# Lookup steps counted by their share of a tile, T1 issued half a slot sooner, blended values written out by ScalarE

## The chip, the cores and the metric

One core of a Trainium2 chip runs the kernel. The metric is the device time of one execution in microseconds (us), as the median of several runs. The engines are TensorE (PE, with its weight loads as PEld), VectorE (DVE), ScalarE (ACT), GpSimd (POOL) and SyncE (SP). DMAs are issued by an engine's queue: SPq is SP's, ACTq is ACT's.

## The reference

Eight sequences of 1024 tokens of width 512 are normalized, go through an attention with three decays and a gated FFN whose weights come out of a 16-entry table, and the product of both is added to the input.

```python
def attn(x, Wq, Wk, Wv, Wo, Wg, decay_logits, out_scale):
    q = x @ Wq
    gate = softmax(x @ Wg)
    expn, causal = maximum(diff - 1, 0), diff > 0      # diff: column minus row
    for i in range(3):
        k, v = x @ Wk[i], x @ Wv[i]
        w = sigmoid(decay_logits[i]) ** expn * causal
        retrieved = einsum('bts,bsd->btd', einsum('btd,bsd->bts', q, k) * w, v)
        blended = blended + gate[..., i:i + 1] * retrieved
    return blended @ Wo * out_scale

def ffn(x, lut, gate_idx, up_idx, down_idx):           # 512 -> 1376 -> 512
    h = silu(x @ lut[gate_idx].T) * (x @ lut[up_idx].T)
    return h @ lut[down_idx].T

xn = layernorm(x)                                      # x: (8, 1024, 512), float32
out = x + attn(xn, ...) * silu(ffn(xn, ...))
```

## The kernel before

Everything is float32. The kernel has two phases. Phase 1 (about the first 597 us) computes the attention up to its blended values and builds the FFN's weights. Phase 2 does the FFN as products in the manner of Strassen (seven products in place of eight, with sums of blocks ahead and behind), the output projection and the final sum; the change doesn't touch it.

**Phase 1 as a loop.** `phase_1` runs a batch counter b from 0 to 8 and in each b eight slots k from 0 to 7. A slot works on chunk c = 7 - k, 128 tokens; chunks go from the last to the first, because the state runs backwards in time. Three streams of work run side by side, each written as a Python generator whose yields mark the places where the other streams get their turn:

- `project(b)`, called newer (and ending for what is left of it in the next b): it loads x by chunk, takes the statistics (for b = 0 on DVE, L404 to L408, otherwise on ACT with junk outputs, L411 and L412, and POOL's power for rstd, L413 and L414), normalizes (L419 on DVE for b = 0, L421 and L422 on ACT otherwise), transposes into xnT (L427, copy L428), makes values pv (L434, copy L437), the gates by a softmax (L440 to L473), and the features q and k by Strassen-like products (`features`, L475 to L535). A gate goes to HBM and comes back spread over all partitions as the tile ga (L473).
- `chunks(b - 1)`, called older: the recurrent attention of the batch before. For each chunk: ga times q on DVE (L627) and qb = ga times a table on POOL (L631); transposes pk of the keys (L643); scores psc (L650) from ga; pr = psc times the decay table on DVE (L652); the state's update pu (L660); the blended output po (L674) from the state and qb, and from pr and the values; a copy of po into the tile bl (L675, ACT). After the eight chunks bl, 128x1024, goes to HBM (bld, L689). The pool of bl has one buffer, so the next batch's first copy waits for that DMA. PSUM tiles pt, pv, pk, psc and po share the three banks of pool p_c.
- `ffn_weights`, called weights: 17 tiles (eleven gate_up, one down_tail, five down). A tile loads its indices (L264 to L266, L317) and looks them up (`look_up`): three bits of the index (L218), the lowest bit spread over the word (L221), eight leaves that select between two table entries (L225), and seven predicated copies that merge them (L242), all on DVE. Then come four sums of 128x256 on POOL (L272 to L276), and for every second gate or down tile four sums over the pair, 128x896 each (L290, L292, L297, L300; L339 to L346). The tile wgu that the last leaf level writes has two buffers, and the pair sums read the wgu of both tiles. Results go to HBM through SP's queue (quadd, L298 and L301). The indices of the following tile are loaded one tile ahead.

In `features`, T1 is the difference of two blocks of xnT, `t1 = b12 - b11` (L505, DVE). T2, T3 and T4 are at L509, L514 and L520. The product pe (L495) reads T1.

**The order.** The generators' turns set the order in which instructions are traced, and for PE, DVE, ACT and POOL `keep_order` holds each engine to this order. SP's order is left to the scheduler. `defer(n, ...)` puts a DMA off by n calls of `tick`, of which a slot has three. `build_some(n)` draws n steps from weights, three times in each slot; before the change a step is one yield, whatever the instruction behind it costs. Yields with nothing between them (three behind a gate pair, eight behind a down pair) are pauses in the lookup.

Of the kernel before, what the change touches and what calls it, by code (L numbers as in the profile page):

```python
# [48 lines left out]
def recurrent_block(ctx: ExitStack, tc, x, wq, wk, wv, wo, wg, decay_logits, out_scale, lut, gidx, uidx, didx, out):  # L49
# [163 lines left out]
    def look_up(build, dst, iv, rows, n):  # L213

        bits = [build.tile([P, n], U8, name=f"bit{j}", tag=f"bit{j}") for j in (1, 2, 3)]
        low = iv.bitcast(U8).rearrange("p (n four) -> p n four", four=4)[:, :, 0]
        for j in (1, 2, 3):
            nc.vector.tensor_scalar(bits[j - 1][:rows, :n], low, 1 << j, None, ALU.bitwise_and)  # L218
            yield

        nc.vector.tensor_scalar(iv, iv, 31, 31, ALU.logical_shift_left, ALU.arith_shift_right)  # L221
        yield

        def leaf(o, k):
            nc.vector.tensor_scalar(  # L225
                o.bitcast(I32),
                iv,
                lut_x[:rows, k, :],
                lut_i[:rows, k, 0:1],
                ALU.bitwise_and,  # L230
                ALU.bitwise_xor,
            )

        def tree(o, level, k):
            if level == 0:
                leaf(o, k)
                yield
                return
            t = build.tile([P, n], F32, name=f"leaf{level}", tag=f"leaf{level}")
            yield from tree(o, level - 1, k)  # L240
            yield from tree(t[:rows, :n], level - 1, k + (1 << (level - 1)))
            nc.vector.copy_predicated(o, bits[level - 1][:rows, :n], t[:rows, :n])  # L242
            yield

        yield from tree(dst, 3, 0)

    def ffn_weights(build, pool, pair_pool):
# [9 lines left out]

        def gate_up(o):
# [8 lines left out]
            yield  # L267
# [6 lines left out]
            yield  # L274
# [16 lines left out]
            yield  # L291
            nc.gpsimd.tensor_tensor(pair[:, :, 1], pair[:, :, 0], b11, ALU.subtract)  # L292
            yield
            if o >= 4 * NQ:
                for _ in range(4):
                    yield
            nc.gpsimd.tensor_tensor(b21, b11, b21, ALU.subtract)  # L297
            defer(3, lambda: nc.sync.dma_start(out=to[:, :, 2:4, :], in_=low))  # L298
            yield
            nc.gpsimd.tensor_tensor(pair[:, :, 2], b12, pair[:, :, 1], ALU.subtract)  # L300
            defer(4, lambda: nc.sync.dma_start(out=to[:, :, 4:7, :], in_=pair))  # L301
            for _ in range(3):
                yield

        def down_tail():
# [3 lines left out]
            yield  # L309
# [4 lines left out]
        def down(rows, e, ends):  # L314
# [3 lines left out]
            yield  # L318
# [5 lines left out]
            yield  # L324
# [15 lines left out]
            yield  # L340
            nc.gpsimd.tensor_tensor(b12, b22, b12, ALU.subtract)
            defer(2, lambda: nc.sync.dma_start(out=to[:, :, 0:2, :], in_=up))
            yield
            nc.gpsimd.tensor_tensor(pair[:, :, 1], b22, pair[:, :, 0], ALU.subtract)
            yield
            nc.gpsimd.tensor_tensor(pair[:, :, 2], b21, pair[:, :, 1], ALU.subtract)  # L346
            defer(4, lambda: nc.sync.dma_start(out=to[:, :, 4:7, :], in_=pair))
            for _ in range(8):
                yield
# [4 lines left out]
        yield  # L354
# [22 lines left out]
    def project(b, pools, sides, kept):  # L377
# [97 lines left out]
        def features(hf):  # L475
# [5 lines left out]
            qk[hf] = att.tile([P, NI + 1, U], F32, name=f"qk{b}_{hf}", tag=f"qk{hf}", bufs=1)  # L481
            c11, c12, c21, c22 = (qk[hf][:, 2 * j : 2 * j + 2, ts(c, H)] for j in (0, 1) for c in (0, 1))
            ts_ = tp.tile([P, 4, 2, H], F32, name=f"ts{b}_{hf}", tag=f"ts{hf}")
            b11, b12, b21, b22 = (xnT[:, 2 * v : 2 * v + 2, ts(2 * hf + c, H)] for v in (0, 1) for c in (0, 1))
            t1, t2, t3, t4 = (ts_[:, k] for k in range(4))
            a11, a12, s3, a22 = (wqk_sb[:, 2 * v : 2 * v + 2, ts(j, 2 * D)] for j in (0, 1) for v in (0, 1))
# [18 lines left out]
            nc.vector.tensor_tensor(t1, b12, b11, ALU.subtract)  # L505
            yield
# [56 lines left out]
        for k in range(NC):  # L563
# [11 lines left out]
            if k == NC // 2:  # L575
# [3 lines left out]
                of_half = features(1)  # L579
                next(of_half)  # L580
# [8 lines left out]
            if k >= NC // 2:  # L589
                next(of_half, None)  # L590
            yield
        of_half = features(0)
        for k in range(NC // 2):
            yield
            if k == 0:
                next(of_half)
# [17 lines left out]
    def chunks(b, pools, kept):  # L614
# [74 lines left out]
        (nc.scalar if at_end else nc.sync).dma_start(out=bl_d[b], in_=bl)  # L689

    def phase_1():
        nonlocal small, p_a, p_c, p_r
        with (
# [22 lines left out]
            def build_some(n):  # L716
                for _ in range(n):
                    next(weights, None)
# [12 lines left out]
            for b in range(B + 1):  # L731
                following = project(b + 1, pools, sides, kept) if b + 1 < B else iter(())
                older = chunks(b - 1, (chk, blp), kept) if b else iter(())
                for k in range(NC):


                    if b == 0:
                        steps = (k > 0, k >= NC // 2, 2 * (k >= NC // 2))
                    elif b < B:
                        steps = ((1, 1, 4), (1, 2, 5), (1, 2, 4), (1, 2, 3))[k % 4]  # L740
                    else:
                        steps = (1, 0, 0)
# [7 lines left out]
                    build_some(steps[0])  # L750
# [6 lines left out]
                    build_some(steps[1])  # L757
                    next(older, None)
                    build_some(steps[2])
# [681 lines left out]
```

## Time and profile before

| | us |
|---|---|
| median of 3 runs | 2113.19 (2112.64 to 2113.54) |
| the profiled execution | 2114.02 |
| its span, first to last instruction | 2111.9 |
| DVE busy in 0 to 597 | 511.23 |
| PE busy in 0 to 597 | 581.45 |
| POOL busy in 0 to 597 | 301.82 |
| ACT busy in 0 to 597 | 373.91 |
| PE busy in 597 to 2112 | 1507.20 |

The profile is one execution on the chip. A time row such as `349.10 0.65 SPq L689 ...` gives the start and the length in us from the span's start, the engine, the line of the code, the operation and its operands as output<-input, and the number of instructions put together. In brackets stands how long the engine was idle before and what released it. A waits row gives engine, tile and line, what it waited for, then the total in us, how many times, and the longest. A group's row ends in busy us, mean ns, and idle time with its releasers.

The costliest groups of the lookup and its neighbours on DVE between 60 and 597 us, in groups of one shape, and of POOL before 597 us:

```profile
L242 DVE COPY_PREDICATED leaf<-bit,leaf 128x1024 f32<-128x1024 uint8 x56 | 81.8, 1460 | 1.2
L225 DVE TENSOR_SCALAR leaf<-idx,lut_x,lut_sb 128x1024 int32<-128x1024 int32 x97 | 81.4, 859 | 0.0
L627 DVE TENSOR_TENSOR ga<-ga,qk 128x384 f32<-128x384 f32 x61 | 44.5, 730 | 2.6 <-DMA ga<-gTd 2.6
L218 DVE TENSOR_SCALAR bit<-idx 128x1024 uint8<-128x1024 uint8 x39 | 40.2, 1068 | 0.0
L652 DVE TENSOR_TENSOR pr<-psc,w_tab 128x384 f32<-128x384 f32 x62 | 34.2, 552 | 36.2 <-PE psc L650 36.2
```

```profile
L631 POOL TENSOR_TENSOR qb<-ga,q_tab 128x384 f32<-128x384 f32 x56 | 79.0, 1410 | 55.0 <-DVE ga L627 49.0 <-PE pe L495 3.6 <-issue 1.7
L300 POOL TENSOR_TENSOR pair<-wgu,pair 128x896 f32<-128x896 f32 x5 | 11.9, 2380 | 0.0
L297 POOL TENSOR_TENSOR wgu<-wgu 128x896 f32<-128x896 f32 x5 | 11.1, 2216 | 0.0
L275 POOL TENSOR_TENSOR wgu<-wgu 128x256 f32<-128x256 f32 x10 | 11.2, 1120 | 0.0
```

### The profile page before, as it was taken

How to read it: one execution, taken by the hardware profiler on the slowest of the kernel's cores; microseconds unless marked ns; L12 is line 12 of the kernel's file. 1: busy time of each engine (PE TensorE's matmuls, PEld its weight loads, DVE VectorE, ACT ScalarE, POOL GpSimd, SP SyncE). 2: the span in 40 equal slices, each digit the busy share in tenths (PEclk: the TensorE clock that was granted, in tenths of full speed). 3: DMA queues.
4: the chain of work that ended last, by engine and by line, in shares of the span. 5: the costliest groups of instructions: out<-in, count | busy, mean ns of one | idle time of the engine just before them, and what ended most of it. 6: DMA issues, size and time to landing. Idle time of an engine off the chain costs nothing.

```text
span 2111.9 us, 32189 instructions
## 1 busy us (share of the span) xinstructions
PE 2088.6 (99%) x11691; PEld 1752.9 (83%) x11691; DVE 1444.2 (68%) x2214; ACT 943.6 (45%) x2116; POOL 1040.4 (49%) x1050
## 2 busy tenths in 40 slices
PE   9999999999999999999999999999999999999999
PEld 7877878888878888887878888887978888797877
DVE  8889897889735675575567556656755665675567
ACT  4766666676434424423441442344144324423531
POOL 4554564364445447516543751655275255527432
PEclk9999999999999999999999999999999999999999
DMA  8765779657864744464454446345544634464442
GB/s 217 146 180 165 188 176 199 161 153 138 157 204 150 256 155 159 162 223 142 157 196 174 157 147 245 136 155 173 197 160 151 248 123 153 160 223 147 150 155 108
DMA packets 184635, 361.51 MB, mean 171 GB/s; under 512 B 50927, under 2 KB 122238, under 8 KB 184478
## 3 DMA queue, kind: packets, MB, share of 16 engines
q1 hardware_dynamic: 169894, 335.20, 52.7%
q0 software_dynamic: 4480, 14.68, 1.7%
q10 hardware_dynamic: 10104, 9.58, 1.5%
q8 instruction: 93, 1.52, 0.3%
q14 instruction: 64, 0.52, 0.1%
HBM read 282.87 MB, written 76.55 MB: 170 GB/s over the span
## 4 chain that ended last, share of the span: by engine, by line
PE 76%; DVE 3%; DMA 1%; issue 0%; ACT 0%; SPq 0%; DVEq 0%; ACTq 0%
PE s L885 33%; PE sE L885 6%; PE s12d L1139 5%; PE s21d L1139 5%; PE s11d L1139 5%; PE fs L833 3%; PE pd L1252 3%; PE ps L1259 3%; PE sEd L1139 2%; PE fsE L833 1%; PE pv L434 1%; PE s11d L1150 1%; PE s21d L1150 1%; PE s12d L1150 1%; PE sEd L1150 1%; PE po L674 1%
## 5 line engine op out<-in xcount | busy, mean ns | idle before, releaser
L885 PE MATMUL s<-xs,wq 128*128 128x256 f32 x3264 | 731.2, 379 | 0.0
L885 PEld LDWEIGHTS s<-xs,wq 128*128 128x128 f32 x3264 | 619.5, 190 | 95.9 <-issue 8.4
L908 DVE TENSOR_TENSOR s<-s,e 128x512 f32<-128x512 f32 x136 | 95.1, 699 | 204.4 <-ACT s L907 204.3
L1223 POOL TENSOR_TENSOR cu<-cu 128x256 f32<-128x256 f32 x32 | 35.1, 1097 | 306.4 <-DVE cl L1222 306.4
L434 PE MATMUL pv<-wvg_sb,xnT 128*128 128x387 f32 x512 | 177.6, 488 | 0.0
L816 POOL TENSOR_TENSOR xs<-xs 128x256 f32<-128x256 f32 x224 | 170.9, 789 | 8.1 <-PE fs L833 3.5
L912 DVE TENSOR_TENSOR sE<-s,e 128x512 f32<-128x512 f32 x136 | 95.0, 698 | 104.6 <-PE s L885 104.6
L976 POOL TENSOR_TENSOR u<-u,e 128x512 f32<-128x512 f32 x64 | 79.9, 1270 | 148.8 <-DVE u L972 130.3
L903 ACT COPY e<-sE 128x512 f32<-128x512 f32 x136 | 79.6, 585 | 138.8 <-PE sE L885 138.5
L885 PE MATMUL sE<-xs,wq 128*128 128x256 f32 x544 | 139.6, 379 | 0.0
L434 PEld LDWEIGHTS pv<-wvg_sb,xnT 128*128 128x128 f32 x512 | 94.4, 191 | 53.9
L980 POOL TENSOR_TENSOR h<-h,u 128x512 f32<-128x512 f32 x64 | 80.1, 1272 | 112.9 <-DVE u L987 100.3
L896 ACT COPY s<-s 128x512 f32<-128x512 f32 x136 | 77.5, 570 | 109.0 <-PE s L885 106.7
L413 POOL TENSOR_SCALAR rstd<-rstd 128x1 f32<-128x1 f32 x56 | 28.8, 515 | 192.3 <-ACT junk L412 186.4
L907 ACT COPY s<-s 128x512 f32<-128x512 f32 x136 | 77.5, 570 | 98.1 <-PE s L885 98.1
L1139 PE MATMUL s12d<-wdd,z 128*128 128x128 f32 x896 | 118.5, 275 | 0.6 <-ACT s12d L1161 0.6
L885 PEld LDWEIGHTS sE<-xs,wq 128*128 128x128 f32 x544 | 103.4, 190 | 14.1
L1139 PEld LDWEIGHTS s12d<-wdd,z 128*128 128x128 f32 x896 | 109.0, 192 | 0.8 <-ACT s12d L1161 0.8
L631 POOL TENSOR_TENSOR qb<-ga,q_tab 128x384 f32<-128x384 f32 x56 | 79.0, 1410 | 55.0 <-DVE ga L627 49.0
L225 DVE TENSOR_SCALAR leaf<-idx,lut_x,lut_sb 128x1024 int32<-128x1024 int32 (+2 forms) x119 | 96.5, 832 | 0.0
L242 DVE COPY_PREDICATED leaf<-bit,leaf 128x1024 f32<-128x1024 uint8 (+2 forms) x68 | 94.2, 1385 | 1.5
L1263 POOL TENSOR_TENSOR gx<-gx,cu 128x512 f32<-128x512 f32 x32 | 40.7, 1277 | 82.0 <-DVE cu L1261 64.5
(263 smaller groups left out, 4534.2 us busy)
## 6 DMA issues: line engine op xcount, KB each, us to landing
wq<-quadd SPq DMA_DIRECT2D x112, 896.0 KB, 4.5
wdd<-wdd SPq DMA_DIRECT2D x56, 896.0 KB, 4.6
xs<-xsd SPq DMA_DIRECT2D x56, 512.0 KB, 6.1
wq<-quadd SPq DMA_DIRECT2D x48, 448.0 KB, 4.1
x<-in_x SPq DMA_DIRECT2D x64, 256.0 KB, 4.7
xsd<-ts SPq DMA_DIRECT2D x16, 1024.0 KB, 14.9
gx<-in_x SPq DMA_DIRECT2D x64, 256.0 KB, 5.3
out<-gx POOLq DMA_DIRECT2D x56, 256.0 KB, 2.3
```

The lines of the kernel that those rows point to most:

```text
L225: nc.vector.tensor_scalar(o.bitcast(I32), iv, lut_x[:rows, k, :], lut_i[:rows, k, 0:1], ALU.bitwise_and, ALU.bitwise_xor,)
L242: nc.vector.copy_predicated(o, bits[level - 1][:rows, :n], t[:rows, :n])
L434: nc.tensor.matmul(pv, lhsT=xnT[:, v, ts(c, P)], rhs=wvg_sb[:, v, :], start=(v == 0), stop=(v == NV - 1))
L816: nc.gpsimd.tensor_tensor(o, x1, x2, ALU.subtract)
L833: nc.tensor.matmul(ps, lhsT=w[:, 2 * W_OF[k] + n, :m], rhs=xs[:, X_OF[k], 2 * n : 2 * n + 2, :], start=start and n == 0, stop=stop and n == 1,
L885: nc.tensor.matmul(self.t[n][:, ts(a, H)], lhsT=self.w[:, a, (0, 1, 6, 3, 4, 5, 2)[i - 1], :], rhs=self.xs[:, X_OF[self.ks[a]], D_OF[i], : ...
L908: nc.vector.tensor_tensor(self.t[1], self.t[1], self.e, ALU.add)
L912: nc.vector.tensor_tensor(self.t[3], self.t[2], self.e, ALU.add)
L976: nc.gpsimd.tensor_tensor(o[:, n], o[:, n], other[:, n], ALU.add)
L980: nc.gpsimd.tensor_tensor(of_h(half, n), of_h(half, n), two(other[:, n]), ALU.mult)
L1139: nc.tensor.matmul(self.t[n][:, ts(a, P)], lhsT=self.lhs[i][:, e, ts(a, P)], rhs=self.w[:, e, D_OF[i], :], start=start and a == 0 and e == ...
L1150: nc.tensor.matmul(self.t[n][:, ts(a, P)], lhsT=self.left[:, ts(2 * (n // 2) + a, P)], rhs=wd_left[:, D_OF[self.k], ts(n % 2, P)], start=F ...
```

## The change

Three things change.

1. A yield of the lookup now carries a number, its share of a tile of 128x1024 (.04 for a bit or the spreading of the lowest, .045 for a leaf, .07 for a predicated copy, .07 or .14 for a POOL sum, nothing for loads). `build_some(part)` adds its part to what is due and draws steps until it is used up, and each of the three places in a slot has a part of its own, by k % 4. The empty yields behind the pairs are gone.
2. T1 and the creation of its tile move ahead of the creation of the feature tile qk, with a yield of their own; the first turn of `features`, which issues T1, is taken at the end of the slot before, so half a slot sooner. For the second half of a batch's features this is the end of the batch's last slot.
3. The DMA that writes bl out is issued by ACT for all batches; before, ACT issued it for the last batch alone, and SP for the other seven.

The number of instructions on PE, DVE, ACT and POOL is unchanged, apart from the DMA's issue. PE's order is the same. ACT's is the same but for the seven DMAs, each directly behind the batch's last copy into bl (L675), and one DMA of the down weights (L328) that comes a few places sooner. DVE's differs in 380 rows, POOL's in 96, and SP's in 106.

```diff
@@ -212,14 +212,18 @@
 
     def look_up(build, dst, iv, rows, n):
 
+        part = n / NB
         bits = [build.tile([P, n], U8, name=f"bit{j}", tag=f"bit{j}") for j in (1, 2, 3)]
         low = iv.bitcast(U8).rearrange("p (n four) -> p n four", four=4)[:, :, 0]
         for j in (1, 2, 3):
             nc.vector.tensor_scalar(bits[j - 1][:rows, :n], low, 1 << j, None, ALU.bitwise_and)
-            yield
+            yield 0.04 * part
 
         nc.vector.tensor_scalar(iv, iv, 31, 31, ALU.logical_shift_left, ALU.arith_shift_right)
-        yield
+        yield 0.04 * part
 
         def leaf(o, k):
             nc.vector.tensor_scalar(
@@ -234,13 +238,13 @@
         def tree(o, level, k):
             if level == 0:
                 leaf(o, k)
-                yield
+                yield 0.045 * part
                 return
             t = build.tile([P, n], F32, name=f"leaf{level}", tag=f"leaf{level}")
             yield from tree(o, level - 1, k)
             yield from tree(t[:rows, :n], level - 1, k + (1 << (level - 1)))
             nc.vector.copy_predicated(o, bits[level - 1][:rows, :n], t[:rows, :n])
-            yield
+            yield 0.07 * part
 
         yield from tree(dst, 3, 0)
 
@@ -254,6 +258,8 @@
 
         upper = []
+        SUM, WIDE_SUM = 0.07, 0.14
 
         def gate_up(o):
             s, m = OCH[o]
@@ -264,14 +270,14 @@
             nc.sync.dma_start(out=iv[:, 2:6, :], in_=gs)
             nc.sync.dma_start(out=iv[:, 0:2, :], in_=us[:, 0:2, :])
             nc.sync.dma_start(out=iv[:, 6:8, :], in_=us[:, 2:4, :])
-            yield
+            yield 0.0
             wf = pool.tile([P, 2 * NB], F32, name="wgu", tag="wgu", bufs=2)
             yield from look_up(build, wf[:, :n], idx[:, :n], P, n)
             w = wf[:, : 2 * n].rearrange("p (k two m) -> p k two m", two=2, m=m)
             a21, a11, a12, a22, s1, s2, s3, s4 = (w[:, k] for k in range(8))
             nc.gpsimd.tensor_tensor(s1, a21, a22, ALU.add)
             nc.gpsimd.tensor_tensor(s2, s1, a11, ALU.subtract)
-            yield
+            yield SUM
             nc.gpsimd.tensor_tensor(s3, a11, a21, ALU.subtract)
             nc.gpsimd.tensor_tensor(s4, a12, s2, ALU.subtract)
             wide = wf[:, 2 * m : 2 * n].rearrange("p (a b) -> p a b", b=m)
@@ -288,25 +294,24 @@
             nc.sync.dma_start(out=to[:, :, 0:2, :], in_=up)
             b21, b22, b11, b12 = low[:, :, 0], low[:, :, 1], up[:, :, 0], up[:, :, 1]
             nc.gpsimd.tensor_tensor(pair[:, :, 0], b21, b22, ALU.add)
-            yield
+            yield WIDE_SUM
             nc.gpsimd.tensor_tensor(pair[:, :, 1], pair[:, :, 0], b11, ALU.subtract)
-            yield
+            yield WIDE_SUM
             if o >= 4 * NQ:
                 for _ in range(4):
-                    yield
+                    yield SUM
             nc.gpsimd.tensor_tensor(b21, b11, b21, ALU.subtract)
             defer(3, lambda: nc.sync.dma_start(out=to[:, :, 2:4, :], in_=low))
-            yield
+            yield WIDE_SUM
             nc.gpsimd.tensor_tensor(pair[:, :, 2], b12, pair[:, :, 1], ALU.subtract)
             defer(4, lambda: nc.sync.dma_start(out=to[:, :, 4:7, :], in_=pair))
-            for _ in range(3):
-                yield
 
         def down_tail():
             s, m = OCH[-1]
             idx = build.tile([P, NB], I32, name="idx", tag="idx", bufs=2)
             nc.sync.dma_start(out=idx[:m, :V], in_=didx[s : s + m, :])
-            yield
+            yield 0.0
             wf = pool.tile([P, 2 * NB], F32, name="wgu", tag="wgu", bufs=2)
             yield from look_up(build, wf[:m, :V], idx[:m, :V], m, V)
             defer(2, lambda: nc.sync.dma_start(out=wdt_d, in_=wf[:m, :V]))
@@ -315,13 +320,13 @@
             idx = build.tile([P, NB], I32, name="idx", tag="idx", bufs=2)
             for a, row in enumerate(rows):
                 nc.sync.dma_start(out=idx[:, ts(a, V)], in_=didx[ts(row, P), :])
-            yield
+            yield 0.0
             t = pool.tile([P, 2 * NB], F32, name="wgu", tag="wgu", bufs=2)
             yield from look_up(build, t[:, : 2 * V], idx, P, 2 * V)
             b11, b12, b21, b22, t1, t2, t4 = (t[:, ts(k, V // 2)] for k in range(7))
             nc.gpsimd.tensor_tensor(t1, b12, b11, ALU.subtract)
             nc.gpsimd.tensor_tensor(t2, b22, t1, ALU.subtract)
-            yield
+            yield SUM
             nc.gpsimd.tensor_tensor(b12, b22, b12, ALU.subtract)
             nc.gpsimd.tensor_tensor(t4, b21, t2, ALU.subtract)
             if e is None:
@@ -337,21 +342,19 @@
             to = wd_d[:, :, e, :].rearrange("p k (t m) -> p k t m", m=P)
             defer(3, lambda: nc.sync.dma_start(out=to[:, :, 2:4, :], in_=low))
             nc.gpsimd.tensor_tensor(pair[:, :, 0], b12, b11, ALU.subtract)
-            yield
+            yield WIDE_SUM
             nc.gpsimd.tensor_tensor(b12, b22, b12, ALU.subtract)
             defer(2, lambda: nc.sync.dma_start(out=to[:, :, 0:2, :], in_=up))
-            yield
+            yield WIDE_SUM
             nc.gpsimd.tensor_tensor(pair[:, :, 1], b22, pair[:, :, 0], ALU.subtract)
-            yield
+            yield WIDE_SUM
             nc.gpsimd.tensor_tensor(pair[:, :, 2], b21, pair[:, :, 1], ALU.subtract)
             defer(4, lambda: nc.sync.dma_start(out=to[:, :, 4:7, :], in_=pair))
-            for _ in range(8):
-                yield
 
         jobs = [gate_up(o) for o in range(NO)] + [down_tail()]
         jobs += [down((j, j + 4), j % 2, j > 1) for j in (0, 2, 1, 3)] + [down((8, 9), None, True)]
         next(jobs[0])
-        yield
+        yield 0.0
         for job, following in zip(jobs, jobs[1:] + [iter(())]):
             next(following, None)
             yield from job
@@ -478,11 +481,13 @@
 
-            qk[hf] = att.tile([P, NI + 1, U], F32, name=f"qk{b}_{hf}", tag=f"qk{hf}", bufs=1)
-            c11, c12, c21, c22 = (qk[hf][:, 2 * j : 2 * j + 2, ts(c, H)] for j in (0, 1) for c in (0, 1))
             ts_ = tp.tile([P, 4, 2, H], F32, name=f"ts{b}_{hf}", tag=f"ts{hf}")
             b11, b12, b21, b22 = (xnT[:, 2 * v : 2 * v + 2, ts(2 * hf + c, H)] for v in (0, 1) for c in (0, 1))
             t1, t2, t3, t4 = (ts_[:, k] for k in range(4))
+            nc.vector.tensor_tensor(t1, b12, b11, ALU.subtract)
+            yield
+            qk[hf] = att.tile([P, NI + 1, U], F32, name=f"qk{b}_{hf}", tag=f"qk{hf}", bufs=1)
+            c11, c12, c21, c22 = (qk[hf][:, 2 * j : 2 * j + 2, ts(c, H)] for j in (0, 1) for c in (0, 1))
             a11, a12, s3, a22 = (wqk_sb[:, 2 * v : 2 * v + 2, ts(j, 2 * D)] for j in (0, 1) for v in (0, 1))
             s1, s2, s4 = (wqs[:, k] for k in range(3))
             lhs = {1: a11, 2: a12, 3: s4, 4: a22, 5: s1, 6: s2, 7: s3}
@@ -502,8 +507,6 @@
                         )
 
             there = xs_d[b][:, :, ts(hf, H)]
-            nc.vector.tensor_tensor(t1, b12, b11, ALU.subtract)
-            yield
             product(pa, 1, True)
             nc.scalar.copy(pb, pa)
             nc.vector.tensor_tensor(t2, b22, t1, ALU.subtract)
@@ -576,8 +579,6 @@
                 if lag:
                     values(c + 1)
                     lag = 0
-                of_half = features(1)
-                next(of_half)
             if k >= NC // 2:
                 next(of_half)
             half = softmax(1) if k == NC // 2 else iter(())
@@ -588,12 +589,12 @@
                 values(c + lag)
             if k >= NC // 2:
                 next(of_half, None)
-            yield
-        of_half = features(0)
+            if k in (NC // 2 - 1, NC - 1):
+                of_half = features(k // (NC // 2) ^ 1)
+                next(of_half)
+            yield
         for k in range(NC // 2):
             yield
-            if k == 0:
-                next(of_half)
             next(of_half)
             half = softmax(0) if k == 0 else iter(())
             next(half, None)
@@ -686,7 +687,7 @@
                     nc.scalar.mul(pu[:, i, :], pu[:, i, :], c_tab[:, i : i + 1])
                 state = new
             yield
-        (nc.scalar if at_end else nc.sync).dma_start(out=bl_d[b], in_=bl)
+        nc.scalar.dma_start(out=bl_d[b], in_=bl)
 
     def phase_1():
         nonlocal small, p_a, p_c, p_r
@@ -713,9 +714,13 @@
             wqs = wts.tile([P, 3, 2, 2 * D], F32, name="wqs", tag="wqs")
             sides = (wvg_sb, wqk_sb, wqs)
 
-            def build_some(n):
-                for _ in range(n):
-                    next(weights, None)
+            due = 0.0
+            def build_some(part):
+                nonlocal due
+                due += part
+                while due > 0.0:
+                    due -= next(weights, 1.0)
 
             write_banks()
             warm_up(4)
@@ -735,11 +740,11 @@
 
                     if b == 0:
-                        steps = (k > 0, k >= NC // 2, 2 * (k >= NC // 2))
+                        parts = (0.05 * (k > 0), 0.05 * (k >= NC // 2), 0.1 * (k >= NC // 2))
                     elif b < B:
-                        steps = ((1, 1, 4), (1, 2, 5), (1, 2, 4), (1, 2, 3))[k % 4]
+                        parts = ((0.05, 0.05, 0.18), (0.05, 0.1, 0.26), (0.05, 0.1, 0.25), (0.05, 0.1, 0.2))[k % 4]
                     else:
-                        steps = (1, 0, 0)
+                        parts = (0.05, 0.0, 0.0)
                     tick()
                     next(newer, None)
 
@@ -747,16 +752,16 @@
                         next(following, None)
                     next(older, None)
                     next(setup, None)
-                    build_some(steps[0])
+                    build_some(parts[0])
                     next(more, None)
                     tick()
                     if k < NC // 2:
                         for _ in range(2):
                             next(ending, None)
                     next(newer, None)
-                    build_some(steps[1])
+                    build_some(parts[1])
                     next(older, None)
-                    build_some(steps[2])
+                    build_some(parts[2])
                     if k < NC // 2:
                         next(ending, None)
                     tick()
```

## The prediction

> **What bounds the kernel now.** I read the page first, then the table of busy time by stretch, then who waits for whom, then the order of time around single waits.
>
> ```profile
> PE 2088.6 (99%) x11691; PEld 1752.9 (83%) x11691; DVE 1444.2 (68%) x2214; ACT 943.6 (45%) x2116; POOL 1040.4 (49%) x1050
> PE 76%; DVE 3%; DMA 1%; issue 0%; ACT 0%; SPq 0%; DVEq 0%; ACTq 0%
> 240.00:300.00 60.00, 58.50 (x341) 48.99 (x340) 58.84 (x66) 38.31 (x101) 37.01 (x30) 1.00 0.74 153
> 300.00:360.00 60.00, 57.40 (x319) 47.50 (x318) 53.76 (x71) 39.59 (x105) 32.73 (x29) 0.97 0.84 215
> 600.00:1000.00 400.00, 398.98 (x2201) 337.42 (x2200) 241.98 (x392) 154.87 (x304) 205.25 (x216) 1.00 0.51 174
> ```
>
> The columns of the last three are length, then busy time (and number) on PE, PEld, DVE, ACT, POOL, then the granted clock. PE has work all the time; the FFN behind 600 us loses next to nothing, and the change leaves it alone. What can be won lies in phase 1, where DVE is 54 to 59 us of 60 busy in the two stretches shown: almost a second bound. The matmul order is the same before and after, so I measure PE's losses as start-to-start spacing above the usual (111 ns for 128 columns, 215.5 for 256, 324 for 387). Their sum is 26.2 us in phase 1. What the losses wait for:
>
> ```profile
> PE po L674 <- DVE pr L652: 9.1, 9, 1.8
> PE pe L495 <- DVE ts L505: 2.1, 3, 0.9
> PE psc L650 <- ACT bl L675: 1.8, 1, 1.8
> DVE wgu L225 <- POOL pair L300: 8.0, 3, 3.0
> ```
>
> (total, times, longest.) The first two are DVE coming late; lookup rows stand ahead of pr and of T1. The third starts as a DMA in a queue:
>
> ```profile
> 346.01 0.53 SPq L298 DMA_DIRECT2D quadd<-wgu  x1
> 348.49 0.52 SPq L301 DMA_DIRECT2D quadd<-pair  x1
> 349.10 0.65 SPq L689 DMA_DIRECT2D bld<-bl  x1
> ...
> 342.83 0.27 ACT L675 COPY bl<-po 128x128 f32<-128x128 f32 x1 [0.86 <-PE po L674]
> ...
> 355.65 0.27 ACT L675 COPY bl<-po 128x128 f32<-128x128 f32 x1 [4.84 <-DMA bld<-bl]
> ```
>
> bl is complete at 343.1, but SP issues its DMA at 349.1, behind two that wait for POOL's sums. The next batch's first copy into the single bl buffer waits for it, po's bank stays taken, PE loses 2.0 us.
>
> **Removed.** By spacing, the losses that the new order takes away:
> - po waits for pr or a bank: .23+1.99+.98+1.53+1.67+1.11+1.13+.60+.26+.92+.59 = 11.0 us (at 98 to 452 us; the view's 9.1 counts idle only, spacing adds the restart).
> - T1 (124, 198, 493 us): 1.04+.54+1.00 = 2.6. With T1 half a slot sooner, DVE has it before PE asks.
> - a wait for qb behind POOL (155): .57.
> - bld: in the new order ACT issues it straight behind the last copy, at 343 instead of 349. That saves the 2.01 us and, behind it, seven 256-column matmuls .21 us too long each (clock .52 from 356.7 to 360.2): 1.5. Together 3.5.
>
> ACT pays for 7 more DMA issues: its DMA of L689 shows .33, that of L466 .60, so 2.3 to 4.2 us in all, hidden because ACT idles about 2 us and more in each slot (2.02 us ahead of 350.32). Should that cover fail, PE waits for xnT; upper end 4.2, I take 0. Queued behind the issue is L428's xnT copy, whose reader comes 5 us later. The added wait on ACT: before issuing, it waits for an earlier DMA of that queue to finish; worst is the ga load issued at 484.5, landing about 491.5, against 489.4: 2.1 us, covered likewise. SP loses 7 issues; nothing behind them waits on SP's time, so 0.
>
> At this clock dip a page and the rows differ. Here a 2.0-us wait (354) preceded clock .52, while 1.99 us at 98 and 1.80 at 597 show 1.00. The Trainium skill, "TensorE: Matmul & The Clock Gate", section "Why this matters for your kernels", asks only for no PE gaps above some 3 us. By it, one of the new waits below (4.75) would cost a dip, 1.5 us more; by the rows, up to four could, 6 us, or none. The sum takes none.
>
> **Added.** The number of lookup instructions is unchanged; a tile of 128x1024 is 4 small operations at about 1.08, 8 leaves at .86, 7 predicated copies at 1.46 us, 21 us of DVE. They change places. I took the new order of DVE and POOL and laid the rows' own durations end to end, each instruction starting when its engine is free and its inputs are there; PE's need is its traced time, less waits already removed, plus waits already added. The same addition with the old order returns the traced waits to about .1 us each, the few that ride on DMAs aside. Three places in full:
>
> (a) Start, 14.57: PE transposes x_4, which DVE normalized at 12.19.
>
> ```profile
> 12.19 0.55 DVE L419 TENSOR_SCALAR x<-x,mean,rstd 128x512 f32<-128x512 f32 x1 [0.32 <-POOL rstd L407]
> ...
> 14.92 0.69 DVE L218 TENSOR_SCALAR bit<-idx 128x1024 uint8<-128x1024 uint8 x1 [1.12 <-DMA idx<-in_uidx]
> ...
> 14.57 0.60 PE L427 MATMUL pt<-ident,x 128*128 128x128 f32 x4
> ```
>
> In the new order two bits stand ahead of that normalizing, and the first can't start before the indices land, at 14.92 here. Two at .66 each, then .55: x_4 at 16.8, so 2.2 us lost. SP's three loads of the second tile's indices now stand ahead of the qk weights (.43+.58+.47 = 1.5 us); the same wait of PE covers them, uncovered they would cost up to 1.5.
>
> (b) Batch starts. T1, and one or two leaves, now stand ahead of ga (L627), which psc of the next batch's first chunk needs.
>
> ```profile
> 268.83 0.86 DVE L627 TENSOR_TENSOR ga<-ga,qk 128x384 f32<-128x384 f32 x1
> 269.61 1.21 DVE L505 TENSOR_TENSOR ts<-xnT 128x512 f32<-128x512 f32 x1
> ...
> 272.22 0.83 PE L650 MATMUL psc<-ga,qk 128*128 128x128 f32 x6
> ```
>
> At 272.22, 10.8 us of waits are gone and 6.0 are new: PE needs ga at 267.4. DVE's new line: two leaves to 268.2, T1 to 269.5, ga to 270.3: 2.85 us. Likewise 1.99 (122), .81 (196), 1.88 (420), .30 (492): 7.8 in all.
>
> (c) Pair sums. Three empty steps behind L300 are gone, and lookups reach the wgu buffer that L300 still reads. POOL at 284 to 298 (new order): L275, L276, L290 (2.2), qb (1.4), L292 (2.2), L297 (2.2), rstd (not before ACT's statistics at 294.2), L300 (2.4 mean), done 298.1. DVE has its bits by 294.5 and stands 3.7 us at the leaf; pr queues behind it. pr is done at 306.9, PE needs it at 302.2: 4.75 lost. At 371 the same: DVE stands 3.4, PE loses 2.04. At 226 DVE stands 5.3, and PE has slack. Behind these and between: .43+.25+.28+.61+.66+.19+.80 = 3.2. Together 10.0.
>
> **Sum.** -11.0 -2.6 -.6 -3.5 + 2.2 + 7.8 + 10.0 = +2.3. On the profiled execution's 2114.02 (span 2111.9 and 2.1 around it) that gives 2116.3; that execution is .8 above the median, so 2115.5 for the median. Bounds: durations vary with company (the L505 row above took 1.21, at 196.98 it took .69), so (b) and (c), 17.8, may be half or, with the waits feeding each other, some 1.4 times: -9 to +7. The rest is firm to 2 us.
>
> **Rivals.**
> - Faster: the removal holds and half of (b)+(c) does not come, since POOL's sums and DVE's rows are shorter while the other stands still (leaf .79 alone against 1.10 to 1.22 beside POOL). 2115.5 - 9 = 2106.5. For it: a DVE at a standstill frees POOL. Against: L413's rstd in (c) waits for ACT, not for speed.
> - Slower: the missing empty steps decide. Place: the first leaf (L225) of the tile behind a gate pair, with pr queued behind. The wait at 226 also reaches PE, at (c)'s 4.75, and a dip of 1.5 follows the longest wait: 2115.5 + 6.3 = 2121.8. It decides once DVE's standstill for L300, 8.0 now, passes about 17 us (my addition has about 15). For: POOL is 37 us of 60 busy in that stretch already. Against: PE's slack at 226.
> - The respreading changes no wait worth the name, and only bld counts: 2113.2 - 3.5 = 2109.7. Against: 380 places differ in DVE's order.
>
> **How the numbers follow.** Forecast: waits change places, 2115.5, own range 2110 to 2119.5, chance .42. Faster rival .29, slower .25, only bld .04. Anything within .2% (4.2 us: 2109.0 to 2117.4) can't be told from no change. Faster: .26 of the faster rival and .01 of the forecast, .27. Slower: .22 of the slower rival and .12 of the forecast, .34. Within: the rest, .39. The range reaches into both rivals: 2104 to 2123.
>
> **What would show it.** In the changed profile: no wait of ACT bl for bld, clock 1.00 at 357; no wait of pe for L505; waits of psc for ga at batch starts (7.8 us, longest 2.9); DVE's wait for L300 at about 15 us instead of 8.0; a first wait of pt near 14.6. I am wrong if po's waits for pr fall well under 8 us, or psc never waits for ga (faster), or if PE loses over 30 us before 600 (slower).

## The result, and the profile after

| | before | changed |
|---|---|---|
| median | 2113.04 us (6 runs, 2112.34 to 2114.45) | 2123.41 us (6 runs, 2121.87 to 2125.05) |
| profiled execution | 2114.02 | 2121.92 |
| its span | 2111.9 | 2120.1 |

The ratio is 1.0048 (95% interval 1.0036 to 1.0061): the change costs 10.4 us, .5%. The prediction said 2115.5 and at most 2123; the true time lies .4 us above that. The changed kernel's six runs fall into two groups of three, 2121.9 to 2122.2 and 2124.7 to 2125.1, and the profiled one belongs to the lower; the upper ones show a mean granted clock of .994 to .995 instead of .996 to .997. What follows explains the 7.9 us between the two profiled executions.

The page of the changed kernel, busy time and the chain that ended last (lines of code are now some 3 to 7 higher: leaves L229, predicated copies L246, the last pair sum L307, T1 L487, ga L628, psc L651, po L675):

```profile
PE 2090.7 (99%) x11691; PEld 1755.2 (83%) x11691; DVE 1438.9 (68%) x2214; ACT 943.9 (45%) x2116; POOL 1028.8 (49%) x1050
PE 83%; DVE 7%; DMA 2%; ACT 2%; POOL 1%; issue 1%; ACTq 0%; SPq 0%; DVEq 0%; POOLq 0%
```

The instruction counts are those of before, and DVE, ACT and POOL are busy for about as long. The waits (PE's first, then DVE's for its lookup buffer; total, times, longest):

```profile
PE po L675 <- DVE pr L653: 10.8, 7, 3.8
PE psc L651 <- ACT ks L647: 3.3, 2, 1.7
PE psc L651 <- ACT pb L511: 2.9, 1, 2.9
PE pt L430 <- DVE x L422: 2.5, 2, 2.0
```

```profile
DVE wgu L229 <- DMA quadd<-wgu: 8.7, 2, 6.5
DVE wgu L229 <- POOL pair L307: 5.0, 1, 5.0
```

T1 and bl are gone from PE's list, as forecast. psc's wait at the batch starts is new and pt's has grown (2.5 in place of .4), as forecast too. Two of the names need the rows in time. Behind psc stands ACT, but these rows show otherwise, here at the start of the second batch (DVE's rows, then PE's, then ACT's):

```profile
118.23 3.28 DVE L222 TENSOR_SCALAR bit<-idx 128x1024 uint8<-128x1024 uint8 x3
121.54 1.10 DVE L225 TENSOR_SCALAR idx<-idx 128x1024 int32<-128x1024 int32 x1
122.67 0.82 DVE L229 TENSOR_SCALAR wgu<-idx,lut_x,lut_sb 128x1024 int32<-128x1024 int32 x1
123.40 0.69 DVE L487 TENSOR_TENSOR ts<-xnT 128x512 f32<-128x512 f32 x1
124.00 0.55 DVE L628 TENSOR_TENSOR ga<-ga,qk 128x384 f32<-128x384 f32 x1
...
124.66 1.62 PE L651 MATMUL psc<-ga,qk 128*128 128x128 f32 x6 [2.86 <-ACT pb L511]
...
123.84 0.60 ACT L511 COPY pb<-pa 128x512 f32<-128x512 f32 x1
```

psc starts .1 us behind the end of ga (124.55). ACT's copy only happens to end (124.44) near that. At the other batch starts it is the same (ga ends at 198.8, 271.8, 428.9, 502.0; psc starts at 198.9, 271.9, 429.0, 502.1). So T1 and five lookup rows ahead of ga make this wait.

The other name was not forecast: DVE stands for a DMA (quadd), not for POOL's sum. Rows of POOL, SP and DVE, the second wait in full and then the first:

```profile
361.74 2.08 POOL L304 TENSOR_TENSOR wgu<-wgu 128x896 f32<-128x896 f32 x1
370.29 2.13 POOL L307 TENSOR_TENSOR pair<-wgu,pair 128x896 f32<-128x896 f32 x1
...
367.43 0.33 SPq L476 DMA_DIRECT2D ga<-gTd  x1
367.86 0.53 SPq L305 DMA_DIRECT2D quadd<-wgu  x1
...
375.96 0.68 DVE L229 TENSOR_SCALAR wgu<-idx,lut_x,lut_sb 128x768 int32<-128x768 int32 x1 [6.54 <-DMA quadd<-wgu]
...
292.85 0.53 SPq L305 DMA_DIRECT2D quadd<-wgu  x1
294.35 2.54 POOL L307 TENSOR_TENSOR pair<-wgu,pair 128x896 f32<-128x896 f32 x1
299.57 0.81 DVE L229 TENSOR_SCALAR wgu<-idx,lut_x,lut_sb 128x1024 int32<-128x1024 int32 x1 [2.12 <-DMA quadd<-wgu]
```

L307 is done at 372.4, yet the first leaf starts at 376.0. It writes the buffer of the pair's second tile, which L305's DMA still reads. The sum that this DMA needs, L304, was done at 363.8; SP issues the DMA at 367.9, behind ga's load, and it takes 8 us. At 299.57 it is the same: L307 is done at 296.9, and the leaf waits for the DMA issued at 292.85. Which buffer a new tile gets is settled when the kernel is built; with the new counting two tiles behind gate pairs (at 299.6 and 376.0) got the one that a DMA holds last.

Last, the clock. A stretch with the first long wait, then the stretches at and right behind the ends of three long waits (the third number from the end is the granted clock):

```profile
118.00:124.60 6.60, 3.43 (x21) 2.87 (x21) 6.53 (x9) 4.54 (x12) 5.15 (x6) 0.99 0.96 339
124.60:128.00 3.40, 3.34 (x11) 3.01 (x12) 3.37 (x7) 0.21 (x1) 0.00 (x0) 0.51 0.74 223
308.70:312.00 3.30, 3.30 (x16) 3.12 (x15) 3.27 (x5) 2.27 (x7) 0.92 (x1) 0.52 0.10 16
377.00:380.50 3.50, 3.34 (x14) 3.27 (x15) 3.47 (x6) 1.56 (x5) 1.30 (x1) 0.52 0.70 265
```

Three times PE runs 3.4 us at half clock. By spacing, matmuls lose 1.4, 1.6 and 1.4 us there, besides what the first matmul behind a wait loses, which is counted with the wait.

PE's losses in phase 1 by spacing, in us:

| | before | forecast | after |
|---|---|---|---|
| pt at 14.5 | 0 | 2.2 | 2.2 |
| psc (before: for bl's copy; after: for ga) | 2.4 | .4 + 7.8 | 8.7 |
| pe for T1 | 2.6 | 0 | 0 |
| po for pr, a bank or qb | 11.6 | 10.0 | 12.7 |
| matmuls at a lower clock, restarts among them | 3.7 | 2.2 | 6.0 |
| fs for a DMA (597, 606 us) | 1.8 | 1.8 | .8 |
| the start and the rest | 4.2 | 4.2 | 3.8 |
| sum | 26.3 | 28.6 | 34.2 |

The sums differ by 7.9, as do the profiled times (2121.92 - 2114.02 = 7.9).

### The profile page after: what moved, and what is told of

It is laid out like the page before. It is cut to its first block, busy times and chain, and to the rows that moved or that the text cites. A ratio compares the mean times of both kernels' runs of the same rounds, so it can differ in the third digit from the quotient of the medians.

```text
span 2120.1 us, 32193 instructions
## 1 busy us (share of the span) xinstructions
PE 2090.7 (99%) x11691; PEld 1755.2 (83%) x11691; DVE 1438.9 (68%) x2214; ACT 943.9 (45%) x2116; POOL 1028.8 (49%) x1050
## 4 chain that ended last, share of the span: by engine, by line
PE 83%; DVE 7%; DMA 2%; ACT 2%; POOL 1%; issue 1%; ACTq 0%; SPq 0%; DVEq 0%; POOLq 0%
PE s L890 33%; PE sE L890 6%; PE s12d L1144 5%; PE s21d L1144 5%; PE s11d L1144 5%; PE fs L838 3%; PE pv L437 3%; PE pd L1257 3%; PE ps L1264 3%; PE sEd L1144 2%; PE po L675 2%; DVE leaf L229 2%; PE pe L500 1%; PE fsE L838 1%; PE s11d L1155 1%; PE s21d L1155 1%
## 5 line engine op out<-in xcount | busy, mean ns | idle before, releaser
L229 DVE TENSOR_SCALAR leaf<-idx,lut_x,lut_sb 128x1024 int32<-128x1024 int32 (+2 forms) x119 | 105.5, 913 | 0.0
L246 DVE COPY_PREDICATED leaf<-bit,leaf 128x1024 f32<-128x1024 uint8 (+2 forms) x68 | 89.2, 1312 | 1.6
```

Source lines behind the costliest of these rows:

```text
L229: nc.vector.tensor_scalar(o.bitcast(I32), iv, lut_x[:rows, k, :], lut_i[:rows, k, 0:1], ALU.bitwise_and, ALU.bitwise_xor,)
```

## The experiments

Each kernel was timed beside the kernel before on the same chip; where kernels from different groups of runs are compared, it is by their ratios to it (.1% is 2.1 us).

**bl's DMA on ACT, alone.** On the kernel before:

```diff
-        (nc.scalar if at_end else nc.sync).dma_start(out=bl_d[b], in_=bl)
+        nc.scalar.dma_start(out=bl_d[b], in_=bl)
```

> The kernel before with one part of the change: ACT issues the DMA of bl for all batches. Theory (the prediction's term bld): the wait of 2.0 us at 354 us and the clock's dip behind it (1.5 us) go, so 3.5 us less than before, 2109.7, with no wait of ACT's bl copy for bld and clock 1.00 around 357. Rival (the issue on ACT costs about what it wins: seven issues of .33 to .60 us and a wait for an earlier DMA of ACT's queue): within 1 us of before, and PE waits behind L428's copy at batch starts.

Measured: 2110.06 against 2113.64, ratio .9985 (.9976 to .9994). The DMA leaves at 343, and the clock stays at 1.00 (rows of ACT, then the same stretch as in the forecast):

```profile
342.76 0.27 ACT L675 COPY bl<-po 128x128 f32<-128x128 f32 x1 [0.85 <-PE po L674]
343.05 0.33 ACTq L689 DMA_DIRECT2D bld<-bl  x1
...
356.70:360.20 3.50, 3.50 (x20) 2.54 (x19) 3.46 (x5) 2.41 (x6) 3.42 (x3) 1.00 0.84 14
```

So the term -3.5 is right, with both halves, wait and clock: 3.6 us by the medians, 3.2 by the ratio.

**T1 sooner, alone.** On the kernel before, the move of L505 and of the turn of `features` as in the change.

> The kernel before with one part of the change: T1 half a slot sooner. Theory: the waits of pe for T1 (2.6 us) go and ga at two batch starts (122 and 196 us, where it had .1 us to spare) is late by T1's .7 each, so about 1.2 us less than before, 2112. Rival (T1 ahead of ga is what makes psc late at batch starts in the changed kernel): psc waits over 4 us in sum, and the time is 2 us or more above before.

Measured: 2111.11, ratio .9988 (.9979 to .9997), 2.5 us less. The waits of pe are gone, and psc waits .5, .6 and .7 us at 122, 196 and 491 us (the third had not been expected). T1 ahead of ga costs 1.8 us there, which is too little for the loss of the changed kernel. The gain is larger than the balance of its waits (2.6 - 1.8 = .8); its profile shows fs losing only .6 us to its DMA, against 1.8, and a dip of 1.7 behind a wait of 2.5 at 98, so single waits elsewhere swing by about as much as this part wins.

**The lookup's new counting, alone.** The changed kernel without the other two parts.

> The changed kernel without its T1 and bld parts, so the lookup's new counting alone. Theory (the new counting makes all of the loss and the other two parts win): above the changed kernel by what bld and T1 win, about 3 to 6 us, so 2126 to 2130, with waits of po for pr near 303 and 373 us of about 4 us each as in the changed kernel. Rival (T1 ahead of ga makes the loss): 2115 or less, since psc no longer waits at batch starts (8.5 us in the changed kernel).

Measured: 2126.5, ratio 1.0059 (1.0046 to 1.0072). The new counting makes the whole loss; whether it makes more lies within the intervals (1.0048 for the changed kernel). So the other two parts win 2.3 us here by the ratios, against 5.1 with the old counting (further down): no wait for bld is left to be removed in this profile, and T1 ahead of ga makes psc later. The waits of PE:

```profile
PE po L677 <- DVE pr L655: 10.1, 6, 5.0
PE pe L498 <- DVE ts L508: 4.2, 5, 1.3
PE psc L653 <- ACT ks L649: 2.3, 1, 2.3
PE psc L653 <- ACT junk L414: 2.2, 3, 1.0
```

Without the move T1 is late by 4.2 us at five batch starts, and psc is late nevertheless (4.5 in this list, 5.1 by spacing, where the changed kernel loses 8.5): whichever stands behind the lookups is late.

**A buffer each for even and odd tiles.** On the changed kernel:

```diff
+        made = []
+        def wgu_tile():
+            made.append(f"wgu{len(made) % 2}")
+            return pool.tile([P, 2 * NB], F32, name=made[-1], tag=made[-1], bufs=1)
-            wf = pool.tile([P, 2 * NB], F32, name="wgu", tag="wgu", bufs=2)
+            wf = wgu_tile()
```

The tiles of down_tail and down are made in the same way.

> The changed kernel with one difference: even and odd lookup tiles have a wgu buffer each, so that the first tile behind a gate pair always writes the buffer of the pair's first tile. In the changed kernel the waits of DVE at 299.6 (2.1 us) and 376.0 (6.5 us) end with the DMA that writes the pair's second tile out (issued 292.9 and 367.9). Theory (the swapped buffer makes DVE wait for a DMA to land in place of POOL's sum): the waits on that DMA are gone, DVE stands 0 to .5 us at 298 and about 3 us at 372, PE's waits there fall from 3.98 to about 2 and from 3.89 to about .5, with their clock dips .5 to 1 less: 5 to 7 us below the changed kernel, 2117 to 2118. Rival (DVE is late there by its queue, whatever the buffer): within 1 us of the changed kernel, 2122.5 to 2124.

Measured: 2117.81, ratio 1.0018 (1.0009 to 1.0027), 5.6 us below the changed kernel by the medians, 6.3 by the ratios. DVE's leaf behind the gate pair starts without a wait at 298.84, and at 372 it waits for POOL's sum, as the forecast had it (3.4 said):

```profile
298.84 1.32 DVE L229 TENSOR_SCALAR wgu<-idx,lut_x,lut_sb 128x1024 int32<-128x1024 int32 x1
...
372.24 0.68 DVE L229 TENSOR_SCALAR wgu<-idx,lut_x,lut_sb 128x768 int32<-128x768 int32 x1 [3.03 <-POOL pair L312]
```

PE's losses fall from 3.98 to 2.51 (305) and from 3.89 to .38 (373), though 1.45 comes at 381. So about half of the loss, or a little more, is the buffer: the forecast had DVE wait there for POOL's last sum alone.

**The first lookups later.** On the kernel with fixed buffers, `0.05 * (k > 1)` for `0.05 * (k > 0)` at b = 0.

> The changed kernel with a wgu buffer each for even and odd tiles (2117.8), and the first lookups of b = 0 one slot later. Theory (the two bits ahead of x_4's normalizing make PE wait for pt at 14.3): that wait (2.2 us in the changed kernel, 2.8 in the one with fixed buffers) goes, and nothing later changes: 2.2 to 4 us less, 2114 to 2115.6. Rival (every lookup is now .05 of a tile later and the later waits move with it): within 1 us of 2117.8.

Measured: 2115.73, ratio 1.0015 (1.0006 to 1.0024): no gain beyond the interval. The wait moved from x_4 to x_3 and grew to 3.7 us, since SP now issues the indices behind the qk weights and they land at 19.6 (rows of DVE):

```profile
19.57 1.30 DVE L222 TENSOR_SCALAR bit<-idx 128x1024 uint8<-128x1024 uint8 x2 [5.69 <-DMA idx<-in_uidx]
20.78 0.54 DVE L427 TENSOR_SCALAR x<-x,mean,rstd 128x512 f32<-128x512 f32 x1
```

So the load has to stay early, and only the bits should move; the kernel of 2102.39 below does that.

**ga and T1 ahead of the last share of lookups at a batch's end.** On the kernel with fixed buffers; `chunks` yields once behind the first `gated`, and in the last slot:

```diff
                     next(older, None)
+                    if k == NC - 1:
+                        if b < B:
+                            upcoming = chunks(b, (chk, blp), kept)
+                            next(upcoming)
+                        tick()
+                        next(newer, None)
                     build_some(parts[2])
...
+                    if k < NC - 1:
-                    tick()
-                    next(newer, None)
+                        tick()
+                        next(newer, None)
```

> The changed kernel with a wgu buffer each for even and odd tiles (2117.8), and at the end of a batch's last slot the order on DVE turned round: first ga of the next batch's first chunk, then T1, then the slot's last share of lookups. Theory (psc at a batch start waits for ga because lookups and T1 stand ahead of it): the waits of psc there (8.5 us, and 1.1 of clock behind the first) fall below 1 us and most of it is won: 2109 to 2112. Rival (DVE simply has more to do there than PE leaves it time for): the waits come back at po for pr of that chunk or at pe for T1 or T2, and the time stays within 2 us of 2117.8.

Measured: 2109.25, ratio .9986 (.9977 to .9995), 6.8 us below the kernel with fixed buffers. psc has left the list; part of it came back at po (10.3 in place of 6.3):

```profile
PE po L681 <- DVE pr L659: 10.3, 14, 2.3
```

**The pauses back.** On the kernel with fixed buffers, behind each gate pair:

```diff
             defer(4, lambda: nc.sync.dma_start(out=to[:, :, 4:7, :], in_=pair))
+            for _ in range(3):
+                yield SUM
```

> The changed kernel with a wgu buffer each for even and odd tiles (2117.8), and behind each gate pair three pauses of .07 of a tile. Theory (the missing pauses bring DVE to the buffer before POOL's last sum is done): DVE's waits for that sum (7.1 us) go, and with them PE's at 305 and 381 (2.5 and 1.4): 3 to 5 us less, 2113 to 2115. Rival (a paused lookup is made up for in the same slots, and pr is late elsewhere): 2117 to 2121.

Measured: 2112.7, ratio 1.0004 (.9995 to 1.0013), 3 us less. DVE no longer stands for the buffer, and PE loses nothing above .25 us at po in all of phase 1. But the lookups end 31 us later, at 591 in place of 560 us, and the FFN waits for the last weights' way through HBM:

```profile
PE fs L845 <- DMA wr<-wgud: 7.7, 1, 7.7
```

So without the pauses po waits and with them it does not, as forecast in (c). The pauses also thin the lookups out over the whole phase; how much of the gain comes from their place and how much from the slower pace was not separated. With them and the same parts the lookups are not done in time.

**bl's DMA on ACT and T1 sooner, with the old counting.**

> The kernel before with two parts of the change, bl's DMA on ACT and T1 sooner, and the lookup steps as before. Theory (the parts add up): 3.6 and 2.5 us less, 2107.5. Rival (with bld's wait gone PE comes sooner, and DVE, late for ga, takes half of it back): 2109 to 2110.

Measured: 2107.19 against 2112.8, ratio .9976 (.9968 to .9985). The two parts add up (-.15 and -.12% alone, -.24% together).

**All repairs.** Fixed buffers, early ga, three pauses, larger parts from b = 4 on, and at the start the indices loaded as early as before with one bit per slot:

```diff
+                    if (b, k) == (0, 1):
+                        next(weights)
-                        parts = (0.05 * (k > 0), 0.05 * (k >= NC // 2), 0.1 * (k >= NC // 2))
+                        parts = (0.04 * (k > 1), 0.05 * (k >= NC // 2), 0.1 * (k >= NC // 2))
...
+                    if 4 <= b < B:
+                        parts = [1.1 * part for part in parts]
```

> All repairs together on the changed kernel: a wgu buffer each for even and odd tiles, ga and T1 ahead of the last share of lookups at a batch's end, three pauses of .07 behind each gate pair, the first bits of b = 0 one per slot as in the kernel before, and from b = 4 on 1.1 times the parts, so that the lookup ends in batch 7 in spite of the pauses. Theory (each named wait was a wait of its own): from the changed kernel's 2123.4 go 5.6 (buffer), 8.6 (batch start), 5.1 (pauses), 2 to 3 (start): 2101 to 2104. Rival (DVE's spare time in phase 1 is used up, and what is taken from one place comes late at another): 2107 or more, with waits of po for pr.

Measured: 2113.75 against 2111.28, ratio 1.0010 (1.0000 to 1.0019), where 2101 to 2104 was expected: a miss, above all by one wait of 7.9 us from 471 on. From 30 to 270 us PE loses not a single wait over .25 us; then in the down tiles DVE stands 6.2 us for the DMA wdd<-wgu.

**The same without pauses and larger parts.**

> The same without the pauses and without the larger parts from b = 4 on. Theory: the kernel with fixed buffers and early ga (2109.25) less the wait of pt at 14 us (2.1): about 2107; PE's waits at 298 and 375 us (2.5 and 1.4) stay. Rival (the indices land late whatever the order): 2109.

Measured: 2102.39 against 2111.28, ratio .9956 (.9943 to .9968). This beats both kernels. Its page, PE's first waits, and DVE's:

```profile
PE 2084.3 (99%) x11691; PEld 1752.7 (83%) x11691; DVE 1431.4 (68%) x2214; ACT 943.0 (45%) x2116; POOL 1036.1 (49%) x1050
```

```profile
PE po L681 <- DVE pr L659: 6.6, 8, 1.7
...
DVE wgu L229 <- POOL pair L312: 12.3, 5, 3.0
DVE wgu L229 <- DMA wdd<-wgu: 0.2, 1, 0.2
```

DVE still stands 12.3 us for POOL's sums. In the changed kernel it stood 13.7 us in all, 5.0 of them for POOL and 8.7 for the DMA; here it is five waits of at most 3.0 us. PE loses 14.8 us in phase 1, against 34.2; no wait of PE for another engine's work reaches 2 us, and no stretch runs at half clock. It fell more than expected (2107). With the lookups' start moved the later waits also came in smaller pieces; which of them is due to what was not separated.

**Early ga on the kernel before.** The kernel with bl's DMA and T1, and the turn of order at a batch's end.

> The kernel before with bl's DMA on ACT, T1 sooner, and ga and T1 ahead of the last lookup steps at a batch's end. Theory: the waits of psc for ga at 122, 196 and 487 us (2.0 us in the kernel with the two parts, 2107.2) go: 2105. Rival (those lookup steps then delay pr): 2107 or more.

Measured: 2108.12, ratio .9984 (.9975 to .9993), not better than without (.9976): the rival. psc's 2.0 us go, but po loses 1.70 in place of .6 at 155 us, where the profile names POOL's qb, and 2.17 in place of 1.57 at 222, where it names DVE's pr. A dip of the clock follows the latter. So the rival's way, by pr, is seen in one of the two.

**Two pauses.** The kernel of 2102.39 with the three pauses behind the third and fourth gate pair alone (`range(3 if o in (5, 7) else 0)`).

> The kernel with fixed buffers, early ga and T1 and one bit per slot at the start (2102.4), and three pauses of .07 behind the third and the fourth gate pair alone (.42 of a tile, some 9 us later at the end of the lookups). Theory (a pause at the place of a wait removes it, and here no speeding up of later parts is needed): PE's waits at 231 (.9) and 297 us (1.8) go, 2099.5 to 2100.5. Rival (what the pauses shift later meets the down tiles' output DMA, as in the kernel with all repairs, where DVE stood 6.2 us for wdd and PE 7.9): above 2103, with a wait of DVE for wdd and of PE for pr near 470 to 545 us.

Measured: 2121.05, ratio 1.0037 (1.0024 to 1.0051): the rival, in full. The waits at 231 and 297 are gone, but at 480 DVE waits for the DMA of a down tile (rows of SP, POOL, DVE):

```profile
468.73 0.33 SPq L483 DMA_DIRECT2D ga<-gTd  x1
469.15 0.53 SPq L350 DMA_DIRECT2D wdd<-wgu  x1
469.77 0.62 SPq L354 DMA_DIRECT2D wdd<-wgu  x1
...
465.32 2.11 POOL L353 TENSOR_TENSOR wgu<-wgu,wgu 128x896 f32<-128x896 f32 x1
...
480.60 0.81 DVE L229 TENSOR_SCALAR wgu<-idx,lut_x,lut_sb 128x1024 int32<-128x1024 int32 x1 [9.75 <-DMA wdd<-wgu]
```

The next down tile writes the buffer that the DMA at L354 reads; the sum was ready at 467.4, SP issued the DMA at 469.8, and the leaf that waits for it starts 10.8 us later, beside other transfers. PE loses 7.3 us by it at 486, with 6.8 us at half clock; the rest of the 17 us above the kernel of 2102.39 (by the ratios) are smaller waits, the largest 3.5 us at 604, and three more dips. In the kernel before, no wait for wdd stands in DVE's list; that the eight empty yields behind the down pairs kept the lookups from that buffer is likely, but no run put them back. Nor was it followed why one tile meets this wait and another does not: in the kernel of 2102.39 it is .2 us.

## Why the prediction was wrong

The places were right and the sum was too small: 2.3 us forecast, 7.9 between the profiles, 10.4 between the medians. Two steps failed. "The sum takes none" put the clock's dips at nothing, and three came, for 4.4 us. And in (c) DVE was to wait for POOL's last sum, while in two of three places it waited for a DMA out of the other buffer, 8.7 us in all; PE's waits at po came to 12.7 us for the 10.0 forecast. The size is near that of the slower rival (2121.8), but by chance: of its mechanism, the wait at 226, PE felt .7 us only. The prediction's own sign of being wrong came, more than 30 us lost by PE before 600: it was 34.2. DVE's standstill, 15 us said and all for L300, was 13.7, of which 5.0 for that sum.

- **Removed: right.** T1's waits are gone in the changed kernel, and alone the move gave 2.5 us. bl's DMA alone gave 3.6 us where 3.5 were said. ACT's seven issues cost .33 to .37 us each, and none of PE's waits in that run points to them.
- **(a) The start: right**, 2.16 us of 2.2.
- **(b) Batch starts: right in sum, in part by luck**, 8.5 of 7.8. The single values were off (3.02, .61, 1.19, 1.80, 1.85 for 1.99, .81, 2.85, 1.88, .30) and made up for each other. At 272 PE came 3.3 us later than summed (270.7 for 267.4) and ga 1.5 us later; at 502 T1 and ga took 1.22 and 1.08 us beside POOL's sums, where they take .68 and .55 at 428. It is the lookups ahead of ga more than T1: with T1 alone moved psc lost 1.8, and with ga and T1 ahead of the lookups the kernel won 6.8.
- **(c) Pair sums: the step that failed in its mechanism.** It said that the leaf waits for the last sum, L300 (L307 now). At 226 that was so (5.0 us, 5.3 said). At 299.6 and 376.0 the tile had the other buffer, and DVE stood 2.1 and 6.5 us for a DMA (3.7 and 3.4 said). The list of what stands behind a tile's buffer has to hold the DMA that writes it out, and the place of that DMA in SP's queue. PE's losses there: 3.98 and 3.89 for 4.75 and 2.04. With fixed buffers 5.6 us were won, and the wait at 372 was for POOL's sum, 3.0 us. All of po came to 12.7 us where 10.0 were said.
- **The clock: the term that was mis-sized most.** The sum took no dip, though the prediction named up to four as its rows' bound; there were three, at the waits of 3.02, 3.98 and 3.89 us, for 1.4 + 1.6 + 1.4 = 4.4 us. With them the forecast's 2115.5 would have been 2120.
- **From the profile to the median** 2.5 us more (10.4 against 7.9) are not explained by waits. The profiled run of the changed kernel is one of the three shorter ones, 1.5 below the median, and that of the kernel before is 1.0 above its own. The lower clock of the longer runs would fit two or three more dips; no profile of such a run was taken, so this stays open.
- **The faster rival fell.** (b) and (c) came to 8.5 + 12.7 = 21.2 us, not to half of 17.8.

## What to carry to other kernels

When work of an engine at its limit is spread anew, ask of each instruction that another engine waits for what now stands ahead of it, and of each buffer what reads it last: here a DMA out of it held it 12 and 13 us beyond the sum that it carries (363.8 to 376.0, 467.4 to 480.6). Empty steps in an order may be what keeps a producer away from such a buffer, so look for new waits when they go. In these runs, waits below 2 us mostly cost PE only themselves, and most of those above cost a dip of the clock too.

## What the runs showed of the hardware

Over the 14 profiles, 32 PE waits from 12 us on lost between 1.4 and 2.0 us by spacing, and one of them was followed by a stretch at half clock (another wait of .7 stood right ahead of it). Of 26 waits that lost more than 2.0 us (2.01 to 7.93), 23 had such a stretch at their end; the exceptions were 2.14 and 2.16 (both near 14 us) and 3.32. By spacing means some .2 us more than the idle time that the views give. One more stretch, in the kernel with the new counting alone, came behind two waits of 1.2 and 1.0 us that ended 1.8 us apart. So the size of a wait alone does not settle it.

Of these 25 stretches, 20 lasted 3.41 us and cost PE 1.6 to 1.7 us beyond the wait, the first matmul behind it included. Five lasted 6.82 us. They stand at waits of 3.46 us and more and began while PE still waited; what was left of them behind the wait cost 1.5 to 3.0 us. The Trainium skill, "TensorE: Matmul & The Clock Gate", section "Why this matters for your kernels", warns of gaps above some 3 us. Here 12 of the 14 waits between 2.0 and 3.0 us were followed by a dip too.
